# Where a two-layer network kernel takes its inverse square roots: from ScalarE with a VectorE reciprocal to a power on GpSimd

## The chip, the core and the metric

The kernel runs on one core of a Trainium2 chip. A core has a matrix engine (TensorE, PE in the profile), three engines for elementwise work (VectorE or DVE, ScalarE or ACT, GpSimd or POOL), a queue that mostly starts transfers (SyncE, SP) and sixteen DMA engines. Each engine takes its own instructions in the order in which they were put into its queue, and semaphores hold an instruction until what it reads is there. The metric is the device time of one execution in microseconds (us).

## The reference

Two layers work on x of 8 batches x 512 tokens x 128 features, all in float32. What matters here are the normalizations:

```python
def _layernorm(x, axis=-1, eps=1e-05):
    m = jnp.mean(x, axis=axis, keepdims=True)
    v = jnp.var(x, axis=axis, keepdims=True)
    return (x - m) / jnp.sqrt(v + eps)

def _rmsnorm(x, w, eps=1e-06):            # in the state-space branch of layer 0, twice
    return x * jax.lax.rsqrt(jnp.mean(x * x, axis=-1, keepdims=True) + eps) * w

h = layer_norm(h, lw, lb)                 # mixture of experts of layer 0: hidden features (512 wide)
return layer_norm(out + x, ln_out_w, ln_out_b)    # and its output (128 wide), eps 1e-6

l2 = jnp.sqrt(jnp.sum(x * x, axis=-1, keepdims=True))     # attention of layer 1
xn = x / jnp.maximum(l2, 1e-12) * scale_norm * gamma      # scale_norm = 128 ** 0.5
```

Layer 0 normalizes x, runs a state-space model (a scan over 512 tokens for 256 channels x 16 states, then an MLP) and a mixture of 24 experts beside it, and adds the product of the two to x. Layer 1 normalizes again, runs causal attention with 8 heads and a mixture of 128 experts, and adds their product.

## The kernel before

Tokens lie on the 128 partitions: a batch of 512 tokens is a tile of 128 x 4 x 128. A normalization gathers its statistics in a small tile, 128 x 4 (one number for each token of a batch) or 128 x 2 for the hidden features, which go two groups of tokens at a time.

The program is written with a tile framework: the source gives the order of the work in the sense of the program, and a scheduler places every instruction in its engine's queue, inserts the semaphores, and, where an activation needs another table than the one that is loaded, a table load ahead of it on ACT.

The stages in the order of time:

- `prepare(b)`, for all batches: load x, layer norm (`ln0`), store the result to `xn_dram`, transpose it, logits of the 24 experts; then `routing()`, which makes the lists of tokens of the experts.
- `expert1` for 24 experts: POOL gathers tokens (L127), PE multiplies, ACT weights the result, SP stores it to `hs_dram`.
- `between()`: for each of 16 pairs of token groups, `begin` fills `hd` with the bias (PE, ACT L431) and POOL adds two gathered rows for each token (L130, an indirect DMA with addition); then the layer norm `lnh` and its weights (DVE L445, L446), and the store to `hid_dram`. `hd` has four buffers, shared with other large tiles.
- `expert2` for 24 experts: POOL gathers hidden rows (L127), PE multiplies, the result goes to `os_dram`.
- `after(b)`: POOL gathers and adds the experts' results into `o` (8 gathers of a batch, L130), layer norm `lno`, its weights on POOL (L483, L484), Silu on ACT (L485), the product with the state-space branch and the sum with x on POOL (L486, L487).
- `Attention.prepare(b)`: layer norm `ln1`, the logits of the 128 experts, the l2 norm `ss2` (POOL L696, DVE L698), the transposed `xaT` with `gamma` as ACT's scale (L708), and `route`, with scatters on POOL (L752).
- `Attention.heads`: scores, softmax, values for 8 heads; at the end the 128 experts (`slots`, `experts`) and `finish`.

The state-space branch (`front`, `scan`, `back`) is a generator whose steps are interleaved with all stages from `expert1` to the attention of the fifth batch. A step of `scan` has exponentials on ACT (`da`, L553), and products and scans on DVE (`u`, L555, L557, L558). `back` holds two normalizations `rms` (POOL L588 squares, DVE L590 sums, DVE L593 scales, POOL L594 multiplies by `n1w`).

Each of the 64 normalizations takes its root on ACT and the reciprocal on DVE: in `norm_stats` at L109 and L110 (40 of them: 8 `ln0`, 16 `lnh`, 8 `lno`, 8 `ln1`), in `rms` at L591 and L592 (16), and for `ss2` at L699 to L702 (8). Only then can DVE scale the data (L116, L446, L593, L703).

Of the kernel before, what the change touches and what calls it, by code (L numbers as in the profile page):

```python
# [8 lines left out]
F32 = mybir.dt.float32  # L9
# [3 lines left out]
AF = mybir.ActivationFunctionType  # L13
ALU = mybir.AluOpType
# [6 lines left out]
P = 128  # L21
B, L, D = 8, 512, 128
NJ = L // P
# [23 lines left out]
def tile_kernel(ctx: ExitStack, tc: tile.TileContext, t: dict, out: bass.AP):  # L47
# [19 lines left out]
    G.affine_select(  # L67
        out=tri, in_=ones, pattern=[[1, P]], compare_op=ALU.is_gt, fill=0.0, base=0, channel_multiplier=-1
    )
    eps5 = const.tile([P, 1], F32, name="eps5")  # L70
    G.memset(eps5, 1e-5)
    eps6 = const.tile([P, 1], F32, name="eps6")
    G.memset(eps6, 1e-6)


    tok_i = const.tile([P, NTT], I32, name="tok_i")
# [21 lines left out]
    def bc(ap, shape):  # L98
        return ap.to_broadcast(list(shape))

    def norm_stats(pool, src, n, eps, tag):

        st = pool.tile([P, n, 6], F32, name=f"{tag}_st")
        mv = pool.tile([P, n, 2], F32, name=f"{tag}_mv")
        for j in range(n):
            V.bn_stats(st[:, j, :], src[:, j, :])
            V.bn_aggr(mv[:, j, :], st[:, j, :])
        rs = pool.tile([P, n], F32, name=f"{tag}_rs")
        S.activation(rs, mv[:, :, 1], AF.Sqrt, bias=eps)  # L109
        V.reciprocal(rs, rs)  # L110
        return mv, rs

    def layernorm(pool, src, dst, n, eps, tag):
# [90 lines left out]
    def prepare(b):  # L204
        xb = xp.tile([P, NJ, D], F32, name="xb")
        Q.dma_start(xb, rows(t["x"][b * L : (b + 1) * L, :]))
        xo = xp.tile([P, NJ, D], F32, name="xo")
        layernorm(st, xb, xo, NJ, eps5, "ln0")
        Q.dma_start(rows(xn_dram[b * L : (b + 1) * L, :]), xo)
        pt = ps_e.tile([P, L], F32, name="pt", tag="pe")  # L210
        for j in range(NJ):
            T.transpose(pt[:, j * P : (j + 1) * P], xo[:, j, :], ident)
        xT = xp.tile([P, L], F32, name="xTp")
        S.copy(xT, pt)
        Q.dma_start(xT_dram[b][:, :], xT)
        pl = ps_e.tile([P, H0, E0], F32, name="pl", tag="pe")
        for h in range(H0):
            T.matmul(pl[:, h, :], xT[:, h * P : (h + 1) * P], wg0, start=True, stop=True)
        V.tensor_copy(lg.rearrange("p (h b) e -> p h b e", b=B)[:, :, b, :], pl)
# [15 lines left out]
    w2 = load(t["mlp_w2"], (P, NJ, D), "w2", w0)  # L235
    b2 = load(t["mlp_b2"].partition_broadcast(P), (P, D), "b2", w0)
    n1w = load(t["norm1_w"].partition_broadcast(P), (P, D), "n1w", w0)
    lno_w = load(t["lno_w"].partition_broadcast(P), (P, D), "lno_w", w3)
    lno_b = load(t["lno_b"].partition_broadcast(P), (P, D), "lno_b", w3)

# [170 lines left out]
    def between():  # L411

        n = 2
        pairs = [(h, b0) for h in range(H0) for b0 in range(0, B, n)]
        begun, affine = [], []

        def begin(h, b0):
            if b0 == 0:  # L420
                lw = me.tile([P, DH], F32, name="lw")
                Q.dma_start(lw, t["lnh_w"][h].partition_broadcast(P))
                lb = me.tile([P, DH], F32, name="lb")
                Q.dma_start(lb, t["lnh_b"][h].partition_broadcast(P))
                affine.append((lw, lb))
            hd = me.tile([P, n, DH], F32, name="hd", tag="big", bufs=4)
            for j in range(n):
                g = h * B + b0 + j
                pb = ps_e.tile([P, DH], F32, name="pb", tag="pe")
                T.matmul(pb, cmbT[:, g, :], eb1, start=True, stop=True)  # L430
                S.copy(hd[:, j, :], pb)  # L431
                gather_add(hd[:, j, :], hs_dram, row[:, g, 0:1])
            begun.append(hd)

        begin(*pairs[0])
        begin(*pairs[1])
        for i, (h, b0) in enumerate(pairs):
            if i + 2 < len(pairs):
                begin(*pairs[i + 2])
            hd, (lw, lb) = begun[i], affine[h]  # L440
            for j in range(n):
                gather_add(hd[:, j, :], hs_dram, row[:, h * B + b0 + j, 1:2])
            mv, rs = norm_stats(st, hd, n, eps6, "lnh")
            for j in range(n):
                V.scalar_tensor_tensor(hd[:, j, :], hd[:, j, :], mv[:, j, 0:1], lw, ALU.subtract, ALU.mult)  # L445
                V.scalar_tensor_tensor(hd[:, j, :], hd[:, j, :], rs[:, j : j + 1], lb, ALU.mult, ALU.add)  # L446
                g = order(h * B + b0 + j)
                Q.dma_start(hid_dram[g * P : (g + 1) * P, :], hd[:, j, :])
            yield
# [19 lines left out]
    def after(b):  # L469

        o = af.tile([P, NJ, D], F32, name="o", bufs=2)
        Q.dma_start(o, rows(xn_dram[b * L : (b + 1) * L, :]))
        sb = af.tile([P, NJ, D], F32, name="sb")
        Q.dma_start(sb, rows(s_dram[b][:, :]))
        xb = af.tile([P, NJ, D], F32, name="xb1", bufs=2)
        Q.dma_start(xb, rows(t["x"][b * L : (b + 1) * L, :]))
        for h in range(H0):
            g = h * B + b
            gather_add(o[:, h, :], os_dram, row[:, g, 0:1])
        for h in range(H0):  # L480
            gather_add(o[:, h, :], os_dram, row[:, h * B + b, 1:2])
        layernorm(st, o, o, NJ, eps6, "lno")
        G.tensor_tensor(o, o, bc(lno_w.unsqueeze(1), (P, NJ, D)), ALU.mult)  # L483
        G.tensor_tensor(o, o, bc(lno_b.unsqueeze(1), (P, NJ, D)), ALU.add)  # L484
        S.activation(o, o, AF.Silu)  # L485
        G.tensor_tensor(o, o, sb, ALU.mult)  # L486
        G.tensor_tensor(xb, o, xb, ALU.add)  # L487
        Q.dma_start(rows(x1_dram[b][:, :]), xb)
        return xb
# [95 lines left out]
    def rms(r, dst, tag):  # L585

        sq = mb.tile([P, NJ, D], F32, name="sq", tag="sq")
        G.tensor_tensor(sq, r, r, ALU.mult)  # L588
        ss = st.tile([P, NJ], F32, name=f"{tag}_ss")
        V.tensor_reduce(ss, sq, AX.X, ALU.add)  # L590
        S.activation(ss, ss, AF.Sqrt, bias=eps6, scale=1.0 / D)  # L591
        V.reciprocal(ss, ss)  # L592
        V.tensor_tensor(dst, r, bc(ss.unsqueeze(2), (P, NJ, D)), ALU.mult)  # L593
        G.tensor_tensor(dst, dst, bc(n1w.unsqueeze(1), (P, NJ, D)), ALU.mult)  # L594

# [32 lines left out]


    gamma = load(t["gamma"], (P, 1), "gamma", w3)  # L630
    wg1 = load(t["wg1"], (P, E1), "wg1", w3)

    mask = w3.tile([P, L], F32, name="mask")
# [30 lines left out]
    class Attention:  # L664
# [6 lines left out]
        def prepare(self, b, xb):  # L671

            at, (ps_x, px) = self.at, self.ps_x
            xn2 = at.tile([P, NJ, D], F32, name="xn2", bufs=1)
            layernorm(st, xb, xn2, NJ, eps5, "ln1")
            pt = ps_x.tile([P, L], F32, name="pt2", tag=px)
            for j in range(NJ):
                T.transpose(pt[:, j * P : (j + 1) * P], xn2[:, j, :], ident)
            xT = at.tile([P, L], F32, name="xT2", bufs=1)
            S.copy(xT, pt)  # L680
            pl = ps_x.tile([P, NJ, E1], F32, name="pl2", tag=px)
            for j in range(NJ):
                T.matmul(pl[:, j, :], xT[:, j * P : (j + 1) * P], wg1, start=True, stop=True)
            lg = at.tile([P, NJ, E1], F32, name="lg2", bufs=1)
            V.tensor_copy(lg, pl)
            for j in range(NJ):
                i = b * NJ + j
                V.max(mx1[:, i, :], lg[:, j, :])
                V.max_index(ix1[:, i, :], mx1[:, i, :], lg[:, j, :])
            bs = slice(b * NJ, (b + 1) * NJ)  # L690
            V.tensor_tensor(lg, lg, bc(mx1[:, bs, 0:1], (P, NJ, E1)), ALU.subtract)
            S.activation(lg, lg, AF.Exp)
            V.tensor_reduce(se1[:, bs], lg, AX.X, ALU.add)

            sq = at.tile([P, NJ, D], F32, name="sq2", bufs=1)
            G.tensor_tensor(sq, xn2, xn2, ALU.mult)  # L696
            ss = st.tile([P, NJ], F32, name="ss2")
            V.tensor_reduce(ss, sq, AX.X, ALU.add)  # L698
            V.tensor_scalar(ss, ss, 1e-24, None, ALU.max)  # L699
            S.activation(ss, ss, AF.Sqrt)  # L700
            V.reciprocal(ss, ss)
            V.tensor_scalar(ss, ss, float(D) ** 0.5, None, ALU.mult)  # L702
            V.tensor_tensor(sq, xn2, bc(ss.unsqueeze(2), (P, NJ, D)), ALU.mult)  # L703
            pt = ps_x.tile([P, L], F32, name="pt3", tag=px)
            for j in range(NJ):
                T.transpose(pt[:, j * P : (j + 1) * P], sq[:, j, :], ident)
            xaT = at.tile([P, L], F32, name="xaT", bufs=3)
            S.activation(xaT, pt, AF.Copy, scale=gamma)  # L708
            self.route(b, xn2)
            return xaT  # L710
# [402 lines left out]
```

## Time and profile before

| | |
|---|---|
| median of 3 runs | 1794.6 us (1783.64 to 1795.8) |
| the profiled execution | 1793.79 us, its span 1792.1 us |
| mean granted TensorE clock in it | 0.845 of full speed |
| table loads on ACT | 165 of 1283 ns |
| roots on ACT (L109, L591, L700) | 64, of 203 to 298 ns in the mean |
| reciprocals on DVE behind them (L110, L592, L701) | 64, of 154 to 170 ns in the mean |
| table loads that stand before a root | 44: 23 at L109, 15 at L591, 6 at L700 |
| indirect DMAs issued by POOL | 400 |

How to read the profile: the page gives the busy time of each engine, and the chain of work that ended last, followed back from the last instruction. A group's line gives the line of the source, the engine, the operation, output and inputs, the count, the busy time, the mean duration, the idle time of the engine just before, and what ended it. "issue" is time for which the profile shows no cause. A table of windows gives busy times stage by stage, since an average over the run mixes stages with different limits. A DMA on POOL is shown for as long as POOL takes to make it, not until the data has landed.

### The profile page before, as it was taken

Reading aid. Unit: us, or ns where it says so; the run is one execution under the profiler, and the core shown is the slowest. Engines: PE = TensorE matmul, PEld = TensorE weight load, DVE = VectorE, ACT = ScalarE, POOL = GpSimd, SP = SyncE. Lnnn points to the kernel's source line nnn. Section 1 sums busy time; section 2 is a strip of 40 time slices with the busy share of each in tenths; the row PEclk is TensorE's granted clock in tenths of the full one; section 3 lists DMA queues with packets and bytes.
Section 4 is the critical chain, followed back from the end, with each engine's and each line's share of the span. In section 5 each row is a group of like instructions: output and inputs, shape, how many; then the busy total and the mean of one; then the engine's idle time right before and its main releaser. Section 6 shows DMA issues by size and latency. Waiting matters only on the chain.

```text
span 1792.1 us, 20555 instructions
## 1 busy us (share of the span) xinstructions
PE 1354.0 (76%) x6921; PEld 938.7 (52%) x6921; DVE 1260.8 (70%) x2778; ACT 928.9 (52%) x1486; POOL 679.5 (38%) x525
## 2 busy tenths in 40 slices
PE   4977787541699973587887797798887857898677
PEld 3744453221587762265564465465565544675455
DVE  6568745667545762468797899799999993665564
ACT  2147664442256752445665465566665554524553
POOL 0037747763644428703412302152252133204630
PEclk9789987555699995698998698799899877998899
DMA  7238978996585564101423221232332211592320
GB/s 247 62 118 271 327 252 170 197 201 152 175 263 155 181 213 91 31 14 57 108 71 94 64 86 65 80 93 65 92 87 83 91 39 32 132 254 74 97 66 18
DMA packets 173755, 222.63 MB, mean 124 GB/s; under 512 B 15578, under 2 KB 115706, under 8 KB 173522
## 3 DMA queue, kind: packets, MB, share of 16 engines
q1 hardware_dynamic: 124626, 101.23, 18.1%
q0 software_dynamic: 30592, 52.98, 14.0%
q10 hardware_dynamic: 18432, 67.12, 11.3%
q8 instruction: 55, 0.90, 0.2%
q14 instruction: 50, 0.41, 0.1%
HBM read 163.40 MB, written 57.80 MB: 123 GB/s over the span
## 4 chain that ended last, share of the span: by engine, by line
PE 30%; DVE 30%; issue 13%; POOL 12%; DMA 8%; ACT 2%; another core or an unknown queue 2%; POOLq 0%; DVEq 0%; SPq 0%; ACTq 0%
DVE u L557 8%; PE po L805 5%; DVE u L555 4%; DVE u L558 4%; PE sc L778 3%; POOL hd L130 3%; DVE sc L780 3%; POOL o L130 3%; PE po L465 2%; PE py L561 2%; DMA hd<-hs_dram,row 2%; PE ph L407 2%; DVE s L816 2%; POOL hg L127 2%
## 5 line engine op out<-in xcount | busy, mean ns | idle before, releaser
L557 DVE TENSOR_TENSOR_SCAN u<-da,u 128x512 f32<-128x512 f32 x256 | 315.7, 1258 | 19.9 <-ACT da L553 13.8
L561 PE MATMUL py<-ident,u 128*128 128x128 f32 x1024 | 168.6, 309 | 115.7 <-DVE u L558 115.7
L561 PEld LDWEIGHTS py<-ident,u 128*128 128x128 f32 x1024 | 135.6, 159 | 164.5 <-DVE u L558 139.2
L805 PE MATMUL po<-v,pT 128*128 128x129 f32 x1280 | 192.6, 297 | 35.0 <-DVE s L816 16.8
L805 PEld LDWEIGHTS po<-v,pT 128*128 128x128 f32 x1280 | 174.9, 208 | 65.4 <-issue 31.2
L555 DVE TENSOR_TENSOR u<-bb,lp 128x1024 f32<-128x1024 f32 x128 | 157.0, 1241 | 72.9 <-PE py L561 17.5
L553 ACT ACTIVATE da<-dt,a_neg 128x512 f32<-128x512 f32 x256 | 175.6, 720 | 49.0 <-DVE u L557 45.6
L778 PE MATMUL sc<-xaT,qm 128*128 128x128 f32 (+3 forms) x512 | 183.5, 464 | 23.2 <-ACT prob L784 18.2
L784 ACT ACTIVATE prob<-sc,mn 128x128 f32<-128x128 f32 (+3 forms) x256 | 131.4, 527 | 121.4 <-DVE mn L780 81.3
L558 DVE TENSOR_TENSOR u<-u,cb 128x1024 f32<-128x1024 f32 x128 | 161.3, 1260 | 3.9 <-DMA cb<-xd_dram 3.0
L780 DVE CUSTOM_DVE_ANT_0 sc<-sc,mask 128x128 f32<-128x128 f32 (+3 forms) x256 | 125.0, 499 | 42.2 <-PE sc L778 30.0
L127 POOL DMA_INDIRECT xg<-xn_dram,inv x72 | 93.5, 1299 | 145.0 <-ACT work L522 112.2
L130 POOL DMA_INDIRECT o<-os_dram,row x64 | 113.1, 1767 | 67.5 <-DMA os_dram<-os 29.8
L130 POOL DMA_INDIRECT hd<-hs_dram,row x64 | 115.4, 1803 | 51.9 <-DMA hd<-hs_dram,row 22.0
L798 PE MATMUL pp<-ident,prob 128*128 128x128 f32 x640 | 113.4, 288 | 22.4 <-ACT pT L800 15.4
L127 POOL DMA_INDIRECT hg<-hid_dram,inv x72 | 87.1, 1210 | 106.2 <-PE pht L460 64.7
L798 PEld LDWEIGHTS pp<-ident,prob 128*128 128x128 f32 x640 | 82.1, 148 | 81.5 <-issue 39.0
L778 PEld LDWEIGHTS sc<-xaT,qm 128*128 128x128 f32 x512 | 84.6, 198 | 66.8 <-ACT prob L784 37.7
L752 POOL DMA_INDIRECT xs_dram<-xn,idx x64 | 76.5, 1195 | 104.7 <-DVE idx L746 42.5
L800 ACT COPY pT<-pp 128x384 f32<-128x384 f32 (+1 forms) x136 | 69.7, 513 | 63.0 <-PE pp L798 55.7
L465 PE MATMUL po<-we,hgT 128*128 128x128 f32 x576 | 83.3, 297 | 0.6 <-ACT hgT L462 0.6
L465 PEld LDWEIGHTS po<-we,hgT 128*128 128x128 f32 x576 | 74.9, 206 | 6.6 <-issue 1.9
(281 smaller groups left out, 2675.3 us busy)
## 6 DMA issues: line engine op xcount, KB each, us to landing
bb<-xd_dram ACTq DMA_DIRECT2D x64, 512.0 KB
cb<-xd_dram ACTq DMA_DIRECT2D x64, 512.0 KB
hs_dram<-hs SPq DMA_DIRECT2D x24, 768.0 KB
we<-in_W SPq DMA_DIRECT2D x48, 256.0 KB
hid_dram<-hd SPq DMA_DIRECT2D x32, 256.0 KB
we<-in_we SPq DMA_DIRECT2D x16, 512.0 KB
os_dram<-os SPq DMA_DIRECT2D x24, 192.0 KB
xb<-in_x SPq DMA_DIRECT2D x16, 256.0 KB
```

What stands on the lines that cost most here:

```text
L127: G.indirect_dma_start(dst, None, table[:, :], IOA(idx, 0))
L130: G.indirect_dma_start(dst, None, table[:, :], IOA(idx, 0), compute_op=ALU.add)
L465: T.matmul(po[:, c, :], hT[:, f, :], we[:, f, :], start=False, stop=(f == NJ - 1))
L553: S.activation(da[:, j, :], dt[:, hf, :], AF.Exp, scale=a_neg[:, hf, n0 + j : n0 + j + 1])
L555: V.tensor_tensor(u, bb, bc(dx[:, hf : hf + 1, :], (P, NC, L)), ALU.mult)
L557: V.tensor_tensor_scan(u[:, j, :], da[:, j, :], u[:, j, :], 0.0, ALU.mult, ALU.add)
L558: V.tensor_tensor(u, u, cb, ALU.mult)
L561: T.matmul(py[:, i, hf * P : (hf + 1) * P], u[:, j, i * P : (i + 1) * P], ident, is_transpose=True, start=False, stop=(n0 + j == DS - 1), ...
L778: T.matmul(sc[:, :w], qm[:, i * P : w], xaT[:, :w], start=True, stop=True)
L780: V.tensor_tensor_reduce(sc[:, :w], sc[:, :w], mask[:, L - w :], -1.0, FMAX, ALU.add, ALU.min, mn[:, i : i + 1])
L798: T.transpose(pp[:, c, :], prob[i][:, k * P : (k + 1) * P], ident)
L805: T.matmul(po[:, i - i0, :], pT[:, i * (i + 1) // 2 + k, :], v[:, k, hd % 4, :], start=(k == 0), stop=(k == i),)
```

## The change

All roots leave ACT. A new helper `rsqrt` takes two instructions on POOL: it adds the epsilon (or takes the maximum with it), and raises the result to the power of -0.5, with a tile `half` that holds -0.5. The reciprocals on DVE go. In `rms` and `ss2` the sum of squares is no longer divided by D, or the result multiplied by sqrt(D): the factor sqrt(D) is multiplied once into `n1w` and `gamma` by DVE, and epsilon is scaled by D instead.

```diff
-    eps5 = const.tile([P, 1], F32, name="eps5")
-    G.memset(eps5, 1e-5)
-    eps6 = const.tile([P, 1], F32, name="eps6")
-    G.memset(eps6, 1e-6)
+
+    half = const.tile([P, NJ], F32, name="half")
+    G.memset(half, -0.5)
...
+    def rsqrt(dst, src, eps, op):
+
+        G.tensor_scalar(dst, src, eps, None, op)
+        G.tensor_tensor(dst, dst, half[:, : dst.shape[1]], ALU.pow)
+
...
         rs = pool.tile([P, n], F32, name=f"{tag}_rs")
-        S.activation(rs, mv[:, :, 1], AF.Sqrt, bias=eps)
-        V.reciprocal(rs, rs)
+        rsqrt(rs, mv[:, :, 1], eps, ALU.add)
         return mv, rs
...
     n1w = load(t["norm1_w"].partition_broadcast(P), (P, D), "n1w", w0)
+    V.tensor_scalar(n1w, n1w, float(D) ** 0.5, None, ALU.mult)
...
         V.tensor_reduce(ss, sq, AX.X, ALU.add)
-        S.activation(ss, ss, AF.Sqrt, bias=eps6, scale=1.0 / D)
-        V.reciprocal(ss, ss)
+        rsqrt(ss, ss, D * 1e-6, ALU.add)
         V.tensor_tensor(dst, r, bc(ss.unsqueeze(2), (P, NJ, D)), ALU.mult)
...
     gamma = load(t["gamma"], (P, 1), "gamma", w3)
+    V.tensor_scalar(gamma, gamma, float(D) ** 0.5, None, ALU.mult)
...
             V.tensor_reduce(ss, sq, AX.X, ALU.add)
-            V.tensor_scalar(ss, ss, 1e-24, None, ALU.max)
-            S.activation(ss, ss, AF.Sqrt)
-            V.reciprocal(ss, ss)
-            V.tensor_scalar(ss, ss, float(D) ** 0.5, None, ALU.mult)
+            rsqrt(ss, ss, 1e-24, ALU.max)
             V.tensor_tensor(sq, xn2, bc(ss.unsqueeze(2), (P, NJ, D)), ALU.mult)
```

The calls of `layernorm` and `norm_stats` pass the number 1e-5 or 1e-6 in place of the tile. In the built program the scheduler puts the instructions of all engines in a new order; ACT is left with 102 table loads of 165.

More of the change, by code (lines that the diff above doesn't have):

```diff
@@ L207, in prepare @@
         xo = xp.tile([P, NJ, D], F32, name="xo")
-        layernorm(st, xb, xo, NJ, eps5, "ln0")
+        layernorm(st, xb, xo, NJ, 1e-5, "ln0")
         Q.dma_start(rows(xn_dram[b * L : (b + 1) * L, :]), xo)
@@ L442, in between @@
                 gather_add(hd[:, j, :], hs_dram, row[:, h * B + b0 + j, 1:2])
-            mv, rs = norm_stats(st, hd, n, eps6, "lnh")
+            mv, rs = norm_stats(st, hd, n, 1e-6, "lnh")
             for j in range(n):
@@ L481, in after @@
             gather_add(o[:, h, :], os_dram, row[:, h * B + b, 1:2])
-        layernorm(st, o, o, NJ, eps6, "lno")
+        layernorm(st, o, o, NJ, 1e-6, "lno")
         G.tensor_tensor(o, o, bc(lno_w.unsqueeze(1), (P, NJ, D)), ALU.mult)
@@ L674, in prepare @@
             xn2 = at.tile([P, NJ, D], F32, name="xn2", bufs=1)
-            layernorm(st, xb, xn2, NJ, eps5, "ln1")
+            layernorm(st, xb, xn2, NJ, 1e-5, "ln1")
             pt = ps_x.tile([P, L], F32, name="pt2", tag=px)
```

## The prediction

> **What bounds the kernel now.** I read the page first: busy shares, then the chain that ended last.
>
> ```profile
> span 1792.1 us, 20555 instructions
> ...
> PE 1354.0 (76%) x6921; PEld 938.7 (52%) x6921; DVE 1260.8 (70%) x2778; ACT 928.9 (52%) x1486; POOL 679.5 (38%) x525
> ...
> PE 30%; DVE 30%; issue 13%; POOL 12%; DMA 8%; ACT 2%; another core or an unknown queue 2%; POOLq 0%; DVEq 0%; SPq 0%; ACTq 0%
> ```
>
> No engine is busy throughout, and ACT, which the change relieves, carries 2% of the chain (some 36 us); POOL, which it loads, carries 12%. Next, the windows by stage, since the limits differ (columns: length; busy us and instructions of PE, PEld, DVE, ACT, POOL; clock, DMA share, GB/s):
>
> ```profile
> 0.00:255.00 255.00, 194.60 (x854) 126.35 (x854) 168.12 (x443) 125.17 (x199) 98.94 (x98) 0.91 0.65 215
> 255.00:450.00 195.00, 101.71 (x221) 47.73 (x220) 120.63 (x195) 81.92 (x115) 119.67 (x69) 0.57 0.83 178
> 450.00:660.00 210.00, 191.65 (x1269) 158.89 (x1270) 117.99 (x104) 117.97 (x218) 94.18 (x77) 0.91 0.63 195
> 660.00:770.00 110.00, 46.42 (x176) 29.45 (x175) 50.66 (x169) 38.31 (x58) 78.32 (x57) 0.63 0.35 81
> 770.00:1480.00 710.00, 572.38 (x2965) 401.00 (x2964) 635.16 (x1295) 421.43 (x653) 198.31 (x132) 0.88 0.25 75
> ```
>
> 770 to 1480 us is DVE's (635 of 710). 450 to 660 is PE's (192 of 210). 660 to 770 is POOL's: 78 us busy, and 17.5 us over the run in gaps of 0.3 between its gathers of o. In 255 to 450 (hidden layer norm) POOL is busy 120 of 195 and DMA 83%; the chain there names POOL's gathers 27% and their landing 19%. Then ACT's groups by form, for the roots:
>
> ```profile
> L109 ACT ACT_TABLE_LOAD x23 | 29.5, 1283 | 8.4 <-DVE ln_mv L107 6.5 <-DVE lnh_mv L107 1.3 <-issue 0.3
> ...
> L591 ACT ACT_TABLE_LOAD x15 | 19.2, 1283 | 0.6 <-DVE u L558 0.3
> ...
> L591 ACT ACTIVATE rms_ss<-rms_ss,eps 128x4 f32<-128x4 f32 x16 | 4.8, 297 | 35.4 <-DVE rms_ss L590 31.1 <-issue 4.2
> ```
>
> 44 loads stand directly before a root (23 + 15 + 6 at L700), and ACT idles in front of roots with its queue blocked: 49.6 us for lnh_mv, 31.1 for rms_ss, 26.8 for lno_mv. The timeline shows one case: ACT sits 6.74 us, though DVE beside it does not stop.
>
> ```profile
> 947.75 1.28 ACT L591 ACT_TABLE_LOAD   x1
> 955.77 0.30 ACT L591 ACTIVATE rms_ss<-rms_ss,eps 128x4 f32<-128x4 f32 x1 [6.74 <-DVE rms_ss L590]
> 956.08 1.28 ACT L502 ACT_TABLE_LOAD   x1
> ```
>
> DVE's waits say how far that reaches. In 770 to 1480 DVE idles 75 us, and none of the waits that are listed with over 1 us ends on ACT; some 40 us end on PE (rsum 12.2, v 10.0, sc 9.6, zm 5.2, pm 2.9), which itself waits 24 us for ACT there (prob 13.7, pT 8.2, qm 2.2).
>
> **What the Trainium skill says.** "ScalarE: Activation LUTs", section "What ACT_TABLE_LOAD costs": about 1283 ns for a load and some 1380 ns of drain beside it. The trace agrees with 1283 ns on every load and shows no drain: above, the root ends at 956.07, the load begins at 956.08 and the next activation stands at 957.38. "Perfetto Trace Analysis", section "Tensor Engine Instruction (MATMUL, LD_WEIGHTS)": the queues of ACT, DVE and GPSIMD are strict FIFO. The waits above agree. "GPSIMD Engine Reference", section "Performance versus the Vector engine", prices a two-input add at 2.6 cycles an element and nothing for a power; the trace's 128x512 products on POOL take 1.26 to 2.27 us.
>
> **The change, part by part.**
>
> *ACT.* 64 roots go (16 x 297 + 16 x 296 + 16 x 296 + 8 x 298 + 8 x 203 ns = 18 us). In the built order table loads fall from 165 to 102, 63 x 1.283 = 81 us. So 99 us of 929 go. Almost none lies on the end: of the chain's entries two are loads, 2.6 us. What can pay is the blocked queue. I give DVE's 40 us of waits on PE in 770 to 1480 a quarter: **-10** (none to 40). PE-bound 450 to 660 holds two rms pairs: **-1**.
>
> *DVE.* 40 reciprocals at L110, 16 at L592, and L699, L701, L702 eight times each go: 6.4 + 2.7 + 1.5 + 1.4 + 2.8 = 14.8 us. In 770 to 1480 it is 1.31 + 1.65 + 0.77 + 1.02 + 2.46 = 7.2 us, of which I count 70% (between DVE's 60% of the chain there and its 89% of the time): **-5**. Two scalings are added, n1w 128x128 (0.28 us, the form of dconv L266) and gamma 128x1 (0.15): under 0.5 us, in the start. n1w's is queued before the last four input layer norms in DVE's order and its load before them in SP's, so I give it no wait.
>
> *POOL.* 64 pairs of a small scalar operation and a power; the power waits for the first. The scalar operation: 0.15 us (memset rows: 128x3 0.18, 128x16 0.13). The power stands in no row and on no page. Below, it costs a memset of one column, 0.09. Above, I take a whole 128x512 product, 1.26: 4 elements then cost 128 times what an element of a product does. I take 0.4, with 0.1 for the wait between the two.
>
> *The wait that the change makes.* DVE works in order, so what counts is how much DVE work the scheduler puts between the statistic and its use. I counted both built orders with durations of the before rows: the median is 4.1 us of other DVE work before and 1.2 us after. The 16 rms uses had 1.4 to 5.5 us in all but one; now all 16 have 1.2 or less and four none. A round trip on POOL is 0.2 (DVE to POOL: 0.08 at 937.21, 0.35 at 933.27) + 0.15 + 0.1 + 0.4 + 0.05 back = 0.9 us. Over all norms the shortfall of cover sums to 6.5 us at a round trip of 0.6, some 14 at 0.9, 36.5 at 1.5 and about 51 at 1.76 (power at 1.26). Before, DVE waited 2.6 us for roots (1.5 + 0.7 + 0.4). At 0.9 some 7 us fall in 770 to 1480 (10 of the 16 rms uses stand there, and I take this 62% for all); eight of the 64 pairs also have a gather or scatter (1.0 to 1.8 us) between their halves, two of them there, 2 us more. 70% of 9: **+6**.
>
> *POOL's queue.* Gathers now stand behind roots. In 255 to 450, 16 pairs x (0.15 + 0.4 + 0.2 for waits and issue) = 12 us, on the path for about half (POOL's gathers with their gaps): **+6**. Against it each hidden norm leaves DVE about 2.7 us earlier (the cover shrinks from 4.1 us in the mean to 1.4), and with four buffers a quarter of 16 x 2.7 = 43 us is on the loop gather, norm, store, gather; DMA at 83% trims it: **-8**. In 660 to 770 eight pairs x 0.75 = 6 us, two thirds on the path, less the load of Silu's table that the chain shows there (1.28): **+3**. Elsewhere POOL is busy 28% in 770 to 1480, and its pairs stand where its product by n1w or lno_w waited already; nobody but DVE waits for them.
>
> *The start.* DVE's lack of cover costs 2 us; in SP's new order the last two loads of x stand before the second filling of xs_dram instead of behind it (they were issued at 40.32, after the fill at 29.83), for which I take -5, since every norm of the start waits for its load: **-3**.
>
> Sum: -10 - 1 - 5 + 6 + 6 - 8 + 3 - 3 = -12 us. The profiled execution took 1793.79 us round a span of 1792.1, 0.8 us below the median, so the 1.7 us around it stay: 1792.1 - 12 + 1.7 = **1782 us**.
>
> **Rivals.**
>
> *ACT was holding the attention back (faster).* The blocking in front of roots delays prob and pT, so PE, so DVE. For it: 141 us of ACT idling at roots (49.6 + 31.1 + 26.8 + 22.4 + 6.8 + 4.3). Against it: 2% of the chain. If DVE's 40 us on PE go by two thirds (-27 for -10) and the power takes 0.15 us (the round trip 0.65: some 4 us less DVE waiting, 3 us less in the gathers), it is 1782 - 17 - 7 = 1758 us.
>
> *The power is dear (slower).* At 1.26 us DVE's shortfall is 51 us, 62% of it in 770 to 1480, 70% of that on the path: +22 for +6. The pairs cost 1.6 us, so +19 for +6 in 255 to 450 (16 x 1.6, three quarters, as POOL then nearly fills that stage) and +7 for +3 in 660 to 770; the start loses 4 more. 1782 + 16 + 13 + 4 + 4 = 1819 us. On that line (37 us for 0.86 us of power, 43 us for one) the gain of 12.6 us is gone at 0.7 us of power, and it is 1% slower from 1.1 us on.
>
> *The change doesn't do what it says.* It does in the built program: no root is left on ACT. But Exp, Silu and Gelu still alternate and keep 102 loads; without the 11 us that I give to ACT, because its queue is then blocked by the next operation instead, it would be 1793 us.
>
> **Numbers.** Forecast 50%, own range 1768 to 1800. ACT rival 23%, dear power 22%, no effect 5%. 1% is 18 us (below 1776.7, above 1812.5), about what can be told from no change. Faster: the ACT rival and two fifths of the forecast, 0.42. Slower: the dear power and a little of the rest, 0.24. Same: 0.34. The range 1750 to 1826 takes in both rivals, and leaves out a power dearer than a whole product or a reordering that helps more than 2.5%.
>
> **What would show it.** ACT's busy time near 830 with 102 loads; a POOL group for the power with its mean (0.4 is the step most in doubt); DVE's waits on POOL for rs and ss near 14 us; 770 to 1480 shorter by some 9 us; hidden norms level; the POOL stage after the experts 3 us longer. A power over 0.7 us with DVE waits over 25 us would prove me wrong, as would DVE's waits on PE falling to half.

## The result, and the profile after

The changed kernel takes **1859.7 us** (median of 4 runs, 1851.0 to 1865.4) against 1792.8 for the kernel before: 1.0378 times as long, interval 1.0319 to 1.0436. It is slower by 67 us, where 12 less were forecast, and lies outside the range of the prediction. The profiled execution took 1851.0 us, span 1849.2.

The page of the kernel after (span; busy us, share and instructions by engine; shares of the chain that ended last):

```profile
span 1849.2 us, 20512 instructions
...
PE 1364.0 (74%) x6921; PEld 942.2 (51%) x6921; DVE 1268.6 (69%) x2701; ACT 834.8 (45%) x1358; POOL 783.1 (42%) x652
...
PE 31%; DVE 30%; POOL 17%; issue 11%; DMA 7%; ACT 3%; another core or an unknown queue 1%; SPq 0%; ACTq 0%; POOLq 0%; DVEq 0%
```

ACT lost 94 of the 99 us that the counts promised (928.9 to 834.8). POOL gained 104 us of busy time and its part of the chain went from 12% to 17%. DVE has 77 instructions fewer, but no less busy time.

POOL's groups by form, for the roots (busy us, mean ns | idle before, releaser):

```profile
L103 POOL TENSOR_TENSOR ln_rs<-ln_rs,half 128x4 f32<-128x4 f32 x16 | 18.3, 1146 | 0.9
L103 POOL TENSOR_TENSOR rms_ss<-rms_ss,half 128x4 f32<-128x4 f32 x16 | 16.7, 1043 | 1.3
...
L103 POOL TENSOR_TENSOR lnh_rs<-lnh_rs,half 128x2 f32<-128x2 f32 x16 | 13.6, 852 | 1.1
...
L102 POOL TENSOR_SCALAR rms_ss<-rms_ss 128x4 f32<-128x4 f32 x16 | 10.0, 623 | 15.6 <-DVE rms_ss L594 15.3
```

A power of 128x4 takes a median of 1.04 us, one of 128x2 a median of 0.72 us: not 0.4. The epsilon takes 0.62 us in the mean at `rms` and 0.46 over all 64, not 0.15. Together the two lines hold POOL for 96 us. DVE's waits (us in total, times, longest):

```profile
DVE hd L450 <- POOL lnh_rs L103: 54.2, 16, 13.4
...
DVE o L119 <- POOL lno_rs L103: 23.6, 8, 8.5
...
DVE xnb L596 <- POOL rms_ss L103: 11.7, 8, 3.0
...
DVE zm L596 <- POOL rms_ss L103: 11.1, 8, 2.5
DVE sq L704 <- POOL ss L103: 10.7, 8, 4.0
```

With `ln1` and `ln0` (6.5 and 5.3 us) that is 123 us of DVE standing for roots, against 2.6 before and 14 forecast. Followed instruction by instruction in the trace, 49 us of it pass before POOL even starts the epsilon, because it is at other work; 7 are the epsilon, 10 lie between epsilon and power, and 55 are the power. The windows of the prediction, in the kernel after:

```profile
0.00:255.00 255.00, 186.94 (x789) 123.72 (x790) 159.82 (x427) 106.44 (x168) 103.54 (x110) 0.80 0.59 196
255.00:450.00 195.00, 106.09 (x263) 49.73 (x260) 101.16 (x148) 66.54 (x95) 138.26 (x102) 0.62 0.84 185
450.00:660.00 210.00, 167.19 (x1081) 136.46 (x1082) 130.31 (x128) 101.50 (x185) 113.02 (x80) 0.84 0.58 182
660.00:770.00 110.00, 51.05 (x301) 42.96 (x299) 47.37 (x90) 29.03 (x53) 64.16 (x52) 0.70 0.46 124
770.00:1480.00 710.00, 564.05 (x2853) 385.06 (x2854) 610.18 (x1221) 377.56 (x591) 250.64 (x194) 0.87 0.25 74
```

They must be read with care, since the stages have moved: 660 us is now still inside the second pass of the experts. Two things can be seen all the same. The hidden-norm stretch has POOL at 138 of 195 us, up from 120; and in 770 to 1480 DVE is busy 25 us less, so it stands more, beside a POOL that is busy 52 us more. Stage by stage, between the first or last POOL gathers and scatters of certain tiles (from the record of each tile's instructions):

| us | before | after | the same order, cheap operations |
|---|---|---|---|
| start, to the first gather of xg | 115.8 | 127.6 | 125.1 |
| first pass of the experts | 147.1 | 153.5 | 150.2 |
| hidden norms | 186.6 | 198.5 | 195.5 |
| second pass | 215.0 | 223.2 | 214.6 |
| first o gather to first xs scatter | 83.9 | 95.6 | 87.7 |
| from there to the last xs scatter | 816.7 | 825.3 | 797.7 |
| the rest | 227.0 | 225.5 | 227.6 |

The third column is the first experiment. Each column is one execution, so a few microseconds of a row mean nothing: the second pass holds only two roots, and its 8 us between the last two columns go with a granted clock of 0.90 and 0.93 there (PE busy 197 and 191 us for the same 1292 matmuls). The loss of 57 us is spread over every stage up to the last scatter: no single wait replaced another.

### The profile page after: what moved, and what is told of

Its sections match the earlier page's. It is cut to its first block, busy times and chain, and to the rows that moved or that the text cites. A ratio compares the mean times of both kernels' runs of the same rounds, so it can differ in the third digit from the quotient of the medians.

```text
span 1849.2 us, 20512 instructions
## 1 busy us (share of the span) xinstructions
PE 1364.0 (74%) x6921; PEld 942.2 (51%) x6921; DVE 1268.6 (69%) x2701; ACT 834.8 (45%) x1358; POOL 783.1 (42%) x652
## 4 chain that ended last, share of the span: by engine, by line
PE 31%; DVE 30%; POOL 17%; issue 11%; DMA 7%; ACT 3%; another core or an unknown queue 1%; SPq 0%; ACTq 0%; POOLq 0%; DVEq 0%
DVE u L561 8%; PE po L806 4%; DVE u L562 4%; POOL hd L133 3%; PE sc L779 3%; DVE u L559 3%; POOL o L133 3%; PE po L469 3%; DVE sc L781 3%; PE ph L411 2%; PE py L565 2%; DMA hd<-hs_dram,row 2%; DVE s L817 2%; PE pht L464 1%; PE pp L799 1%
## 5 line engine op out<-in xcount | busy, mean ns | idle before, releaser
L806 PEld LDWEIGHTS po<-v,pT 128*128 128x128 f32 x1280 | 177.0, 209 | 63.7 <-issue 31.7
L559 DVE TENSOR_TENSOR u<-bb,lp 128x1024 f32<-128x1024 f32 x128 | 161.7, 1280 | 67.8 <-PE py L565 40.1
L781 DVE CUSTOM_DVE_ANT_0 sc<-sc,mask 128x128 f32<-128x128 f32 (+3 forms) x256 | 124.9, 499 | 39.4 <-PE sc L779 30.2
L130 POOL DMA_INDIRECT hg<-hid_dram,inv x72 | 106.2, 1475 | 71.4 <-PE pht L464 39.5
L411 PE MATMUL ph<-we,xTe 128*128 128x512 f32 x144 | 75.5, 665 | 4.6 <-ACT hs L412 2.3
```

Source lines behind the costliest of these rows:

```text
L130: G.indirect_dma_start(dst, None, table[:, :], IOA(idx, 0))
L559: V.tensor_tensor(u, bb, bc(dx[:, hf : hf + 1, :], (P, NC, L)), ALU.mult)
L781: V.tensor_tensor_reduce(sc[:, :w], sc[:, :w], mask[:, L - w :], -1.0, FMAX, ALU.add, ALU.min, mn[:, i : i + 1])
L806: T.matmul(po[:, i - i0, :], pT[:, i * (i + 1) // 2 + k, :], v[:, k, hd % 4, :], start=(k == 0), stop=(k == i),)
```

## Experiments

Three theories. R, round trip: DVE stands until POOL's answer is there. Q, queue: roots and POOL's other work hold each other up. O, order: the new order that the scheduler makes is itself slower. Every group of runs had the kernel before beside it on the same chip. It took 1791 to 1793 us there, but 1774 beside the last three (the controls with cheap operations for the spare pairs and for `rms`, and the constant data), so ratios are compared, and a comparison across groups supposes that they carry over.

**The power left out, the order kept.** In `rsqrt`, the epsilon and the power become two cheap operations, so every root is 0.5:

```diff
-        G.tensor_scalar(dst, src, eps, None, op)
-        G.tensor_tensor(dst, dst, half[:, : dst.shape[1]], ALU.pow)
+        G.tensor_scalar(dst, src, 0.0, None, ALU.mult)
+        G.tensor_tensor(dst, dst, half[:, : dst.shape[1]], ALU.subtract)
```

> The changed kernel with the power left out: the two POOL instructions of every root stay (the scalar one multiplies by 0, the second subtracts -0.5, so every root is 0.5), and the built order of all five queues is the same, row for row. Only the duration of the second instruction changes, from 1.04 us (128x4) and 0.72 us (128x2) to that of an ordinary small operation, which I put at 0.25 us. Theory R (the round trip on POOL is paid by DVE, whose queue has almost no work left between the statistic and its use): some 46 us of POOL time go, nearly all of it from the path: 1815 to 1825 us, and DVE's waits on the second instruction fall from 123 us to about 75. Theory O (it is the new order, with its short cover and all the instructions that moved, and not what the power takes): 1850 us or more. Theory Q (POOL's queue: roots behind gathers and gathers behind roots, in the hidden norms and the output norms): a third of the gain of R, about 1845 us.

Measured: 1810.2 us, ratio 1.0098 (1.0071 to 1.0125), a little below what R gave. Each engine's order is row for row that of the kernel after, so the order and the cheap operations together account for 19 us. The five groups of powers hold POOL for 66.5 us, the cheap operations for 17.2: 49 us less, and the run is 49.5 us shorter. That the two agree so well is partly chance, since the first operations of the pairs took 10 us longer here (39.4 for 29.2). DVE's waits for roots fell from 123 to 88 us: the 49 us before POOL starts a root are still there, and the part of the last operation fell from 55 to 12. The granted clock of the two profiles differs (0.823 and 0.865), but mostly in the start (0.71 and 1.00); in the run with constant data, below, it is 0.849 and the loss is there. Two of those groups in this kernel, to be read beside the same lines of the kernel after:

```profile
L103 POOL TENSOR_TENSOR lnh_rs<-lnh_rs,half 128x2 f32<-128x2 f32 x16 | 5.3, 329 | 1.1
...
L103 POOL TENSOR_TENSOR rms_ss<-rms_ss,half 128x4 f32<-128x4 f32 x16 | 3.2, 201 | 1.3
```

**The epsilon moved to DVE.**

```diff
-        G.tensor_scalar(dst, src, eps, None, op)
+        V.tensor_scalar(dst, src, eps, None, op)
```

> The changed kernel with the addition of epsilon (or the maximum) done by DVE instead of POOL, so POOL has one instruction for each root and nothing can stand between the halves. Theory R: the round trip is shorter by 0.23 us (the undisturbed scalar operation) to 0.6 us and a gap of 0.1, 64 times 0.45 = 29 us, against 64 x 0.16 = 10 us more on DVE: 1838 to 1848 us. Theory Q: the splits by a gather go, which is most of the 54 us of DVE waits in the hidden norms: 1830 to 1840 us. Theory O: the order is new again, so 1850 to 1870 us, with no sign that can be told.

Measured: 1823.1 us, ratio 1.018 (1.0114 to 1.0247), below all three. This is half of the loss back for moving one small instruction of each root, though the order is another too. The hidden norms, where Q looked for the gain, have no part in it: their stage took 199.7 us (198.5 in the kernel after), and DVE stood 55.5 us for `lnh`.

**The hidden norms back on ACT** (`lnh` takes the old square root and reciprocal):

```diff
+        if tag == "lnh":
+            sqrt_recip(rs, mv[:, :, 1], eps6)
+        else:
+            rsqrt(rs, mv[:, :, 1], eps, ALU.add)
```

> The changed kernel with the 16 hidden norms alone back on ACT and DVE (Sqrt and reciprocal); all other roots stay on POOL. 115 table loads instead of 102. Theory R: DVE's 54 us of waits for these roots go, and of the 12 us that the stage of the hidden norms lost all come back: 1843 to 1850 us. Theory Q: the stage and what is queued behind it (the expert stage that follows lost 8 us more) come back: 1835 to 1842 us. Theory O: 1855 us or more.

Measured: 1833.3 us, ratio 1.0201 (1.014 to 1.0262), just below what Q gave. The hidden-norm stage took 187.8 us, as before the change (186.6).

**All 40 layer norms back on ACT**; `rms` and `ss2` stay on POOL.

```diff
-        rsqrt(rs, mv[:, :, 1], eps, ALU.add)
+        sqrt_recip(rs, mv[:, :, 1], eps5 if eps == 1e-5 else eps6)
```

> The changed kernel with all 40 layer norms back on ACT and DVE; only the 16 rms norms and the 8 l2 norms keep their root on POOL. 149 table loads. Theory R: what is left of the loss goes with what is left of DVE's waits for roots, 33.5 of 123 us, so 27% of 67 us: about 1811 us. Theory Q: POOL is free in the gather stages, 1800 us or less. Theory O: any new order with short cover costs, 1835 us or more.

Measured: 1833.0 us, ratio 1.022 (1.0157 to 1.0284). A miss for R and Q: 24 roots alone keep 40 us of the loss, and the 24 norms that went back beyond `lnh` brought nothing. The start is back at 116.0 us, but that `ln0` on POOL is what lengthened it isn't shown: it took 122.6 us in the next kernel, which has no root on POOL, and 115.5 in the one after that, which has.

**No root work at all.** One DVE instruction in place of the pair:

```diff
+        V.tensor_scalar(dst, src, 0.0, 0.5, ALU.mult, ALU.add)
```

> The after kernel with each root replaced by ONE small DVE instruction (times 0, plus 0.5), so no root work on ACT or on POOL at all; sqrt and power are left out, every normalization multiplies by 0.5. This is the most that taking roots off ACT could bring. If my step on ACT was right (-11 us for ACT relief, -3 for the net of DVE's small instructions): 1776 to 1781 us. If ACT's relief is worth nothing (it carried 2% of the chain): 1787 to 1793. If the new orders that the scheduler makes are slower by themselves (theory O): 1800 or more.

Measured: 1790.6 us, ratio 1.0026 (0.9997 to 1.0054). Its page:

```profile
span 1789.1 us, 20421 instructions
...
PE 1357.1 (76%) x6921; PEld 938.0 (52%) x6921; DVE 1260.9 (70%) x2762; ACT 845.1 (47%) x1367; POOL 688.0 (38%) x524
```

ACT has 84 us less to do than before and POOL hardly more, and the kernel is as long as before. DVE's five largest waits for PE in the long attention stage sum to 67.6 us before, 63.6 here and 59.2 after: roots on ACT were not what held PE. In this order there was nothing to gain in all. By stages (one profile each) there are gains and losses: the hidden norms took 177.0 us for 186.6, and the long stage up to the last scatter 808.3 for 816.7, but the start and the stretch from the first o gather to the first scatter took 7 us more each. These 14 us don't come from roots on POOL, since there are none.

**One instruction on POOL.**

```diff
+        G.tensor_scalar(dst, src, 0.0, 0.5, ALU.mult, ALU.add)
```

> The same with the one instruction on POOL in place of DVE (times 0, plus 0.5): the crossing to POOL and back alone, with one short instruction there. Round trip (theory R): between the kernel without any root work and the 1810 us of the kernel with two short POOL instructions, about 1797 us, and DVE's waits for POOL's roots near 55 us of idle time (85 with two). Queue of POOL (theory Q: a root stands behind gathers whatever it lasts): 1807 to 1812, waits as with two. Order (theory O): 1810 or more.

Measured: 1798.7 us, ratio 1.0053 (1.0027 to 1.0078), the time that R gave, but with 70 us of DVE's waits for the roots; 57 of them pass before POOL starts the operation. None, one, two cheap operations, each in its own order: +0.3%, +0.5%, +1.0%.

**The hidden norms alone on POOL**, all else as before.

```diff
+        if tag == "lnh":
+            rsqrt(rs, mv[:, :, 1], 1e-6, ALU.add)
+        else:
```

> The before kernel with only the 16 hidden norms (lnh) made on POOL with the epsilon and the power; all others stay on ACT. One part alone. If parts add up as when lnh was put back (1860 to 1833, 26 us): 1815 to 1820 us. Theory R by DVE's waits (54 us of idle time on lnh after, a third of it on the end): 1805 to 1812. If the hidden norms are covered by gathers and DMA at 83% (what I predicted): 1788 to 1795.

Measured: 1809.3 us, ratio 1.0101 (1.0073 to 1.0129), as R gave by DVE's waits. Its hidden-norm stage took 212.9 us for 186.6, of which the second pass gave 8 back. The timeline of the kernel after shows two ways in which DVE comes to stand (start, duration, engine and instruction, and in brackets the idle time before). In the first, the scheduler put a gather between the epsilon and the power:

```profile
306.57 1.11 POOL L102 TENSOR_SCALAR lnh_rs<-lnh_mv 128x2 f32<-128x2 f32 x1
...
307.94 1.78 POOL L133 DMA_INDIRECT hd<-hs_dram,row  x1 [0.27 <-issue]
309.18 1.31 POOL L103 TENSOR_TENSOR lnh_rs<-lnh_rs,half 128x2 f32<-128x2 f32 x1
310.52 1.42 DVE L450 SCALAR_TENSOR_TENSOR hd<-hd,lnh_rs,lb 128x512 f32<-128x512 f32 x2 [2.28 <-POOL lnh_rs L103]
```

Two operations of 0.23 and 0.72 us take 3.9, and DVE stands for 2.28 us. But only 3 of the 16 hidden norms have a gather there. In the other way, the more costly one, the whole root stands behind gathers:

```profile
393.96 0.18 DVE L111 BATCH_NORM_AGGREGATE lnh_mv<-lnh_st 128x2 f32<-128x6 f32 x1
...
396.75 1.55 POOL L133 DMA_INDIRECT hd<-hs_dram,row  x1 [2.25 <-DMA hd<-hs_dram,row]
398.60 1.55 POOL L133 DMA_INDIRECT hd<-hs_dram,row  x1 [0.30 <-issue]
400.46 1.55 POOL L133 DMA_INDIRECT hd<-hs_dram,row  x1 [0.30 <-issue]
402.09 0.22 POOL L102 TENSOR_SCALAR lnh_rs<-lnh_mv 128x2 f32<-128x2 f32 x1
402.39 0.72 POOL L103 TENSOR_TENSOR lnh_rs<-lnh_rs,half 128x2 f32<-128x2 f32 x1
403.15 1.42 DVE L450 SCALAR_TENSOR_TENSOR hd<-hd,lnh_rs,lb 128x512 f32<-128x512 f32 x2 [7.79 <-POOL lnh_rs L103]
```

The statistic is there at 394.14, and POOL starts the epsilon 8 us later, after three gathers, the first of which waited for a landing. Of the 54.2 us that DVE stands for `lnh`, 34 pass before POOL starts the epsilon, 4.5 between the halves, and 13 in the power. So this wait hardly depends on the power: with cheap operations DVE stood 53.1 us for `lnh`.

**Only the factor sqrt(D) moved into gamma**, roots on ACT: the one part of the change that saves an instruction and adds no wait.

```diff
-            V.tensor_scalar(ss, ss, float(D) ** 0.5, None, ALU.mult)
+    V.tensor_scalar(gamma, gamma, float(D) ** 0.5, None, ALU.mult)
```

> The before kernel with only the factor sqrt(D) of the l2 norm moved into gamma (the eight L702 multiplications go, one of 128x1 comes); all roots stay on ACT. By its DVE time 2.8 us go, five of eight of them in the DVE-bound stage: 1789 to 1792 us, no difference that can be told (ratio 0.997 to 1.001). If the scheduler's new order weighs more than the instruction: anywhere from 1780 to 1810.

Measured: 1786.3 us, ratio 0.9983 (0.9963 to 1.0004, 20 runs). The interval holds 1, so no version is shown to beat the kernel before.

**POOL loaded, nobody waiting.** The root is one DVE instruction; the epsilon and the power go to a spare tile:

```diff
+        V.tensor_scalar(dst, src, 0.0, 0.5, ALU.mult, ALU.add)
+        spare = shade[:, : dst.shape[1]]
+        G.tensor_scalar(spare, dst, eps, None, op)
+        G.tensor_tensor(spare, spare, half[:, : dst.shape[1]], ALU.pow)
```

> The kernel with one small DVE instruction for each root (times 0, plus 0.5, so every normalization multiplies by 0.5 and the roots themselves are left out), and beside it the full pair on POOL, epsilon and power, into a spare tile that nobody reads. POOL's queue is loaded as after the change, but no DVE instruction waits for it. Round trip (theory R: DVE's wait for the answer is what costs): 1790 to 1802 us, close to the 1790.6 us of the kernel without any root work. Queue of POOL (theory Q: the pairs push gathers, scatters and products back): 1825 to 1850 us, most of the way to 1859.7.

Measured: 1841.1 us, ratio 1.0268 (1.0202 to 1.0334). R fails as the only cause: DVE waits for these pairs once, 3.9 us for a buffer, and most of the loss is there. O fails here too: apart from the spare pairs and a stretch of some 35 us in the attention, every engine's order is that of the kernel without root work (1.0026). Nor are DVE's own instructions slowed by the pairs: it is busy 1255.9 us, for 1260.9 there.

**The same with cheap operations**, every engine's order unchanged.

```diff
-        G.tensor_scalar(spare, dst, eps, None, op)
-        G.tensor_tensor(spare, spare, half[:, : dst.shape[1]], ALU.pow)
+        G.tensor_scalar(spare, dst, 0.0, None, ALU.mult)
+        G.tensor_tensor(spare, spare, half[:, : dst.shape[1]], ALU.subtract)
```

> The kernel with the spare pairs on POOL that nobody reads, same built order on every engine, same data, with the two cheap operations in place of epsilon and power. If POOL's queue is what costs (theory Q): the powers' 56 us of POOL time go with most of their effect, 1795 to 1808 us. If the order is slower by itself (theory O): 1830 or more.

Measured: 1787.7 us, ratio 1.0119 (1.0059 to 1.0178), by the ratio somewhat above what Q gave. So 1.5% of the 2.7 is the powers' time on POOL in an order and with data that are the same; the intervals leave 0.2 to 2.7% for it. Some 0.9 more come with the cheap pairs. DVE's waits in the two profiles show where such a delay comes out, here of the kernel with the powers:

```profile
DVE lnh_st L113 <- DMA hd<-hs_dram,row: 72.6, 13, 16.6
DVE u L562 <- PE py L568: 60.0, 9, 14.7
...
DVE ln_st L113 <- POOL xb L494: 35.8, 6, 12.7
```

With cheap operations these are 66.2, 52.5 and 17.5 us. The clearest is the wait for `xb`, the last of POOL's products in `after(b)`, which doubles. POOL's products stand behind the powers, and DVE waits for the products; how much of the 1.5% comes this way was not summed up.

**Only rms on POOL**, and its control with cheap operations in the same order:

```diff
-        S.activation(ss, ss, AF.Sqrt, bias=eps6, scale=1.0 / D)
-        V.reciprocal(ss, ss)
+        rsqrt(ss, ss, D * 1e-6, ALU.add)
```

> The before kernel with only the 16 roots of rms made on POOL (epsilon times D, power, sqrt(D) folded into norm1_w); all layer norms and the l2 norm keep ACT and the reciprocal. One part alone, in the stage that DVE sets. Round trip (theory R): DVE waited 25 us for rms_ss in the kernel with rms and l2 on POOL, which cost 40 us with the eight l2 roots; so 1812 to 1820 us here, and a wait of 20 us or more on rms_ss. Queue of POOL (theory Q; POOL is busy 28% of 770 to 1480): 1791 to 1798. My prediction's own reading (6 us of wait less 5 us of reciprocals less 10 us of ACT's relief): 1780 to 1788.

> The kernel with only the rms roots on POOL, in the same built order on every engine, but with two cheap operations (times 0, minus -0.5) in place of epsilon and power; the rms roots are left out and are 0.5. If the power's time is what costs (theory Q or R: 16 powers, some 0.9 us longer each): of the 44 us about 25 go, 1808 to 1815 us. If the order of this kernel is slower by itself (theory O): 1825 or more.

Measured: 1837.0 us, ratio 1.0232 (1.0176 to 1.0288); the control 1805.2 us, ratio 1.02 (1.0149 to 1.0252). The first is a miss for R and Q, though the wait of 20 us or more that R named is there. By its ratio the control goes with O, and its 16 cheap pairs cost more than all 64 did (1.0098). DVE's waits for the roots, first with the power, then without:

```profile
DVE zm L601 <- POOL rms_ss L107: 11.3, 8, 2.5
...
DVE xnb L601 <- POOL rms_ss L107: 9.9, 8, 1.5
```

```profile
DVE zm L601 <- POOL rms_ss L107: 4.3, 7, 1.6
...
DVE xnb L601 <- POOL rms_ss L107: 3.2, 7, 0.6
```

That is 21.2 and 7.5 us, far from the loss. But how much of it goes with the order is not settled. The two kernels ran on different chips, and up to the last scatter, behind which no root stands, their profiles are 42.7 and 21.5 us longer than before (1607.8 and 1586.6 for 1565.1): by the profiles the powers are half of the loss, by the ratios almost nothing. In either reading 20 us or more are left that 16 cheap pairs, or the order built for them, cost; which place costs was not found. Nor do the parts add up: `lnh` alone on POOL costs 1.0%, but taking it off again gives 1.8 back, and taking the other 24 layer norms off as well nothing.

**Constant data with the power.** The cheap kernels have roots of 0.5, so this one raises a constant 4 to -0.5, in the order of the kernel after:

```diff
-        G.tensor_scalar(dst, src, eps, None, op)
+        G.tensor_scalar(dst, src, 0.0, 4.0, ALU.mult, ALU.add)
```

> The changed kernel in its own built order with the power, but of the constant 4 (times 0, plus 4.0), so every root is 0.5 as in the cheap kernels; the true roots are left out. If the power's time is what costs: 1850 to 1865 us as with true data. If the data did it (0.5 in place of the true roots changes what the later stages do): 1810 to 1820 us.

Measured: 1826.8 us, ratio 1.0312 (1.0245 to 1.0378). With order and data equal, the power against the cheap operations is 1.0312 against 1.0098: 2.1%, some 38 us. The intervals of this run and of the kernel after overlap (1.0319 to 1.0436), so an effect of the data is neither shown nor needed. The profiles say the same: up to the last scatter this kernel took 1621.9 us, the kernel after 1623.7, and the one with cheap operations, of which the fastest of nine runs was profiled, 1570.8. The chip of this run was faster behind the last scatter (204.5 us for 225.5), which the ratio, taken over the whole time, can't set right exactly.

## Why cover did not cover

One place in the attention stage shows what the count of cover missed. First the kernel after:

```profile
888.38 1.22 DVE L559 TENSOR_TENSOR u<-bb,lp 128x1024 f32<-128x1024 f32 x1
888.55 1.13 POOL L102 TENSOR_SCALAR rms_ss<-rms_ss 128x4 f32<-128x4 f32 x1 [0.81 <-DVE rms_ss L594]
...
889.76 1.04 POOL L103 TENSOR_TENSOR rms_ss<-rms_ss,half 128x4 f32<-128x4 f32 x1
...
890.84 0.69 DVE L596 TENSOR_TENSOR xnb<-zm,rms_ss 128x512 f32<-128x512 f32 x1 [1.24 <-POOL rms_ss L103]
```

Then the kernel with the same order and cheap operations:

```profile
861.06 1.21 DVE L559 TENSOR_TENSOR u<-bb,lp 128x1024 f32<-128x1024 f32 x1
861.23 1.12 POOL L102 TENSOR_SCALAR rms_ss<-rms_ss 128x4 f32<-128x4 f32 x1 [0.81 <-DVE rms_ss L594]
...
862.44 0.20 POOL L103 TENSOR_TENSOR rms_ss<-rms_ss,half 128x4 f32<-128x4 f32 x1
...
862.67 0.69 DVE L596 TENSOR_TENSOR xnb<-zm,rms_ss 128x512 f32<-128x512 f32 x1 [0.40 <-POOL rms_ss L103]
```

DVE has one product `u` of 1.2 us between the statistic and its use, just the cover that the prediction counted. But POOL's epsilon starts under that product and ends only some 0.1 us after it: 1.13 us for an operation that takes 0.23 alone. The cover is used up by the operation that it was meant to hide, and the whole power then stands open: 1.24 us of waiting against 0.40. In the kernel after, 23 of the 64 epsilon operations ran beside a DVE instruction with two tensor inputs and took 0.85 us in the mean; the other 41 took 0.23. The Trainium skill, "SBUF — State Buffer", section "Who interferes with whom", says why: "A DVE instruction with two SBUF inputs contends with a GpSimd instruction that reads SBUF", and the order of issue decides which of the two blocks. These durations agree. The prediction did not price it.

## The prediction, step by step

What failed is the part on POOL. The power was put at 0.4 us and took 1.04 (0.72 for 128x2), the epsilon at 0.15 and took 0.46 in the mean, and one wait was put at nothing: a root that stands behind POOL's own gathers and products before it starts. That wait is 49 of DVE's 123 us, and the power 55. The 11 us that ACT was to give did not come either.

- **ACT's relief (-10 and -1).** The counts were right, 102 loads and 834.8 us busy for "near 830". Over the whole the relief was nothing: with the roots gone from ACT and nothing put on POOL the ratio is 1.0026. In one profile of that kernel the long attention stage is 8 us shorter, and other stages lose it again. The 2% of the chain was the right reading. The quarter of DVE's waits on PE rested on PE's waits for ACT, and those were much the same after, 26.3 us for 26.7 in 770 to 1480. And in the case that the prediction shows, DVE does stop, 0.93 us, but for POOL's squares and not for ACT.
- **DVE's removed instructions (-5).** They went, yet DVE's busy time rose from 1260.8 to 1268.6 us, since its other instructions took longer (the first product `u` of a scan step 1.28 us in the mean for 1.24, the scan itself 1.273 for 1.258), and DVE stood more as well. That this would have paid if nothing else had changed isn't shown: one part of it, the fold into gamma, gave a ratio of 0.9983 that can't be told from 1.
- **The power (0.4 us).** Named as the step most in doubt, and it failed: 1.04 us for 128x4. Its own sign of being wrong, a power over 0.7 us with waits over 25, came, with 123.
- **DVE's waits (+6 from 14 us).** Both operations of the round trip were mis-sized, the cover was taken as independent of POOL, and POOL was taken as free when a root comes, but for the eight pairs with a gather or scatter between their halves (these eight are in the trace). In the attention stage DVE stands 36 us for roots, where some 9 were counted.
- **POOL's queue (+6 - 8 and +3).** Hidden norms came out at +12, not level. The gain from DVE's earlier end was real, 10 us in the kernel without root work, but it was eaten by roots that stand behind gathers. With `lnh` back on ACT the stage is at 187.8 us. From the first o gather to the first scatter it is +12 instead of +3; 7 of these are there without any root work and with the layer norms back on ACT (91 us in both), so they go with the order. What the sum lacked besides was POOL's own work in other stages, products and gathers behind a power, which the spare pairs show without any wait for a root.
- **The start (-3).** It is +12, and back at 116.0 us with `ln0` on ACT. Since it is +7 without any root work, and level with one cheap operation on POOL, the order has a part in it that was not separated. The earlier loads of x did not pay for it.
- **The rival that the power is dear** had the right side and, with DVE's shortfall and the pairs' time on POOL, much of the mechanism. Its line of 43 us for each microsecond of power gives 1810 us at 1.04. Measured, the powers are longer by 0.77 us in the mean (49.3 / 64) and cost 38 to 50 us, so 49 to 64 for one; and its starting point was too low by some 35 us, since cheap operations stand at +19 and not at -16 or so.

What stays open: how the 38 to 50 us of the powers divide between POOL's queue and DVE's standing (spare pairs 1.5%, waited for 2.1 to 2.8%, intervals that touch), how much of the remaining 19 us is the order, and what makes `rms` alone so dear.

## What to carry to other kernels

Before moving an operation to another engine to relieve the first, ask what the kernel takes without the operation at all; here, in the order that the scheduler then made, that was no less. When the engine that sets the time waits for a small operation on a side engine, it can pay the full latency, and first of all the wait for what stands ahead in the side engine's queue, as the gathers did here. Cover by a two-input DVE instruction was none for the epsilons that began under it. A duration that stands in no profile is worth a range that goes past the dearest value one can imagine, and its slope must count the work queued behind it too.

## What was unexpected of the hardware

- A power on POOL costs 1.04 us for 128x4 and 0.72 us for 128x2, five and three and a half times the 0.20 us of a subtraction of the same size. A few elements take the time in which POOL squares a whole 128x512 tile, and most of that of a product of two (1.04 and 1.26 us at best).
- A tiny POOL operation beside a two-input DVE instruction lasts until that ends: 0.23 us becomes up to 1.14, and in the kernel with spare pairs one lasted 5.58 us beside several in a row. The other way round, the powers held nobody: in that kernel 31 of DVE's products and scans of `u` began while a power ran and took 1.21 us as they do alone, while 24 that began under a whole 128x512 product of POOL took 2.07 us in the mean.
- The mean granted clock of the four runs with spare powers was 0.820 to 0.827, with cheap spare operations 0.830 to 0.857. In the kernel after it was 0.820 to 0.846 with no relation to the time (1851.0 us at 0.823, 1865.4 at 0.843). Whether powers on POOL lower it isn't settled: between the profiles of the spare pairs most of the difference lies in the start (0.72 and 1.00) and behind the last scatter (0.91 and 0.97), and in the long part between them, which holds most of the roots, it is 0.81 and 0.83.
